# Gated delta attention in a decoder layer: the group's beta in two buffers, the blocks' signs later, squares summed together, w_out scaled on ScalarE, and half of the first inverse on VectorE

## The chip, the core and the metric

The kernel runs on one core of a Trainium2 chip. A core has five engines with instruction lines of their own: TensorE (PE; its weight loads are shown as PEld), VectorE (DVE), ScalarE (ACT), GpSimd (POOL) and SyncE (SP, which issues DMAs here; ACT can issue some too). Each runs its line in order and waits on semaphores for the others. The metric is the device time of one execution in microseconds (us), lower is better. "Span" is the time from the first to the last instruction of the one execution that was profiled.

## What is computed

A decoder layer over 16 sequences (B) of 128 tokens (S) with 256 features: a gated delta attention, a cross attention and a mixture of experts, each followed by a layer norm. All that changes lies in the attention:

```python
mixed = silu(causal_conv4(hidden_states @ w_qkv))      # q, k: 16 heads of 128; v: 32 heads of 128
z     = hidden_states @ w_z
beta  = sigmoid(hidden_states @ w_b)
g     = -exp(A_log) * softplus(hidden_states @ w_a + dt_bias)
q = l2norm(repeat(q, 2)) * 128 ** -0.5                 # 16 heads -> 32
k = l2norm(repeat(k, 2))

def step(Sm, inp):                                     # for each token in turn
    q_, k_, v_, g_, b_ = inp
    Sm = Sm * exp(g_)
    delta = (v_ - einsum('bhk,bhkv->bhv', k_, Sm)) * b_
    Sm = Sm + einsum('bhk,bhv->bhkv', k_, delta)
    return Sm, einsum('bhk,bhkv->bhv', q_, Sm)

og  = o * silu(z)
on  = og * rsqrt(mean(og * og) + 1e-6) * norm_w
x   = layernorm(x + on @ w_out)
```

## The kernel before

**Units and slots.** The recurrence over tokens is done as matrix products. A *unit* is one key head (hk, 16 of them) of one group of G = 4 sequences (g, 4 of them), with its two value heads r = 0, 1: 64 units in all (class Unit). For each unit the 128 tokens are cut into four blocks of 32; within a block a triangular 32x32 matrix has to be inverted, and between blocks there are substitutions. A software pipeline runs over slots `for s in range(NU + DELAY + 3)`. In slot s the unit a = s does its keys and queries (projection pjkq, a convolution over time in ykq, SiLU into kq, the decay scan e from dec, the products pk and lp), v = s - 6 its values (pjv, yv, y2v, vT), m = s - 7 and p = s - 8 their block substitutions (pu) and block products with the inverse (pt), p also its gate (pjz, zs), q = s - 9 the attention (po, og), and o = s - 10 the output (pp, acc).

**Groups and inverses.** Four units with consecutive numbers make a Group (U = 4): 4 units x 2 heads x 4 sequences = 32 blocks in each of four rows of blocks, inverted at once, one block on each partition. `Group.begin` (VectorE) copies the group's beta (bg), transposes it (bp, one buffer), transposes the gathered diagonal blocks (ldg into Tp), and makes nbp = -beta / norm; as its last but one step GpSimd multiplies Tp by nbp (L251), the sign and scale of the blocks. `step(j)`, j = 1 to 30, is two GpSimd operations (L267, L269) on 30 to 240 elements for each partition; `end` sets the diagonal and multiplies by bp (L275); `norms` makes nk (L258); `turn` transposes the result on VectorE into Tt (L279), behind the last lp product of the slot. Group k is inverted in the slots with s // 4 - 1 = k, in the first three of four: each slot has five calls `piece(0)` to `piece(4)`, and the 30 steps are spread over 13 of these 15 pieces. The first pt that uses Tt stands in the slot after.

**Who orders what.** GpSimd's line follows the program text (`manual_schedule` for Pool). The lines of the other engines and of the DMA queues are ordered by a scheduler that estimates times and places an instruction as soon as what it needs is there in that estimate. A buffer's next writer waits for its last reader.

**What stands in a slot, in GpSimd's line:** piece(0); the clear of the lower blocks of lp of unit s - 1 (L417); rstd of o (L478, a power); piece(1), piece(2), the sum of the two conv halves of v (L359, which frees y2v and leads to vT), piece(3), the second such sum, piece(4).

**Sums of squares.** `norms` of a unit squares q (sq), sums over features with a ones matrix into PSUM (pss, L377), transposes (sqt, L380) and makes ss (L382). `rms` does the same for og2 (pms L467, mst L471, var L474, a sum with ss). rstd is var to the power of -0.5, and acc takes pp x rstd.

**w_out.** It has to be scaled by norm_w along rows. `scale_wo(i)`, i = 0 to 7, in slots 2 to 9, loads two heads' rows on SP into a buffer shared with og2, scales on GpSimd (L170) and stores to DRAM (wo_d) on SP; load_o fetches from there.

Of the kernel before, what the change touches and what calls it, by code (L numbers as in the profile page):

```python
# [16 lines left out]
P = 128  # L17
# [24 lines left out]
def decoder_kernel(  # L42
# [16 lines left out]
    ones = const.tile([P, BS], F32, name="ones")  # L59
    pool.memset(ones, 1.0)  # L60
# [56 lines left out]
    with ExitStack() as st:  # L117
# [44 lines left out]
        def scale_wo(i):  # L162

            wor = sb.tile([P, 2, G, P], F32, tag="og2", bufs=1, name=f"wor{i}")
# [49 lines left out]


        NU = NG * HK

        class Group:
# [7 lines left out]
            def begin(self):  # L226
# [11 lines left out]
                self.bp = bp = small("bp", bufs=1)  # L238
# [11 lines left out]

                pool.tensor_tensor(self.T, self.T, bc(nbp[:, None, :], [P, BS, BS]), ALU.mult)  # L251
                sst = small("sst", bufs=1)
                vec.transpose(sst, ss)
                self.sst = sst

# [6 lines left out]
            def step(self, j):  # L262
# [14 lines left out]
            def turn(self, after):  # L277
                self.Tt = sb.tile([P, 8 * U, BS], F32, tag="Tt", name=f"Tt{self.k}")
                inst = vec.transpose(self.Tt.rearrange("p q t -> p t q"), self.T)  # L279
                if after is not None:  # L280
                    tc.add_manual_dep(inst.ins, after.ins.name, mybir.DependencyInfo(
                        mybir.DependencyClass.NoSync, mybir.DependencyReason.DATA),
                        reason="behind what VectorE can do before GpSimd is done")

        class Unit:


            def __init__(self, n):
                self.g, self.hk = divmod(n, HK)
                self.n, self.u = n, n % U  # L290
                self.bt = slice(self.g * G, (self.g + 1) * G)
# [46 lines left out]
            def conv(self, name, ws, chunk, out=None):  # L338
# [10 lines left out]
                for k in (2, 1, 0) if out is not None else (1, 0):  # L349
                    d = 3 - k  # L350
                    vec.scalar_tensor_tensor(  # L351
                        out=y[:, :, d:], in0=pj[:, :, : P - d], scalar=c[:, k : k + 1],
                        in1=y[:, :, d:], op0=ALU.mult, op1=ALU.add)
                if out is not None:
                    act.activation(out, y, AF.Silu)
# [14 lines left out]
            def norms(self):  # L370

                sq = self.t([P], "sq", bufs=1)
                act.activation(sq, self.kq[:, :, 1, :], AF.Square)
                pss = sm_pool.tile([P, G, BS], F32, tag="sm", name=f"pss{self.n}")
                for i in range(NB):
                    blk = slice(i * BS, (i + 1) * BS)
                    pe.matmul(pss[blk].rearrange("p b t -> p (b t)"), lhsT=ones, rhs=sq[:, :, blk],  # L377
                              start=True, stop=True)
                sst = self.t([BS], "sqt", bufs=1)
                vec.transpose(sst, pss)  # L380
                self.ss = self.t([], "ss", bufs=DELAY + 5)
                vec.tensor_scalar(self.ss, sst[:, :, 0], 1e-6, 1e-6 * P, ALU.add, ALU.mult)  # L382

            def decay(self):

                self.e = []
                for r in range(2):
                    e = self.t([P], "e", r)
                    vec.tensor_tensor_scan(  # L389
                        out=e.rearrange("p b t -> p (b t)"), data0=self.dec[:, r, :],  # L390
                        data1=ident4.rearrange("p b t -> p (b t)"), initial=0.0,
                        op0=ALU.mult, op1=ALU.add)
                    self.e.append(e)
# [56 lines left out]
            def attend(self, r):  # L450

                if r == 0:
                    self.og = self.t2("og")
                    self.og2 = self.t2("og2", bufs=1)
# [5 lines left out]
                act.activation(self.og2[:, r], self.og[:, r], AF.Square)  # L460

            def rms(self):

                pms = sm_pool.tile([P, 2, G, BS], F32, tag="sm", name=f"pms{self.n}")
                for i in range(NB):
                    blk = slice(i * BS, (i + 1) * BS)
# [813 lines left out]
```

## Time and profile before

| | us |
|---|---|
| median of 3 runs | 2245.6 (2243.43 to 2249.56) |
| the profiled execution: its time | 2240.06 |
| the profiled execution: its span | 2238.0 |
| start of slot 7 / slot 12 / slot 63 (scan at L389) | 136.8 / 256.8 / 1604.2 |
| w_out's scaling on POOL (L170), 8 times | 22.8 (2.85 each) |
| 480 + 480 operations of the steps on POOL (L267, L269) | 245.6 + 265.8 |
| pss on PE / sqt on DVE / pms on PE / mst on DVE, 64 units | 27.9 / 20.0 / 49.4 / 28.8 |
| granted TensorE clock, mean | 0.969 |

The attention fills the span to about 1800 us; the cross attention and the experts, which the change leaves as they are, follow. In the profile's lists a line reads: place in the kernel and engine, operation, the tile written and those read, shape, count, and in square brackets the idle time just before and what ended it. In the list of waits it reads: the waiting group <- what ended the wait, then total us, number of times and the longest.

### The profile page before, as it was taken

The numbers are of one execution on the slowest core, as the hardware profiler recorded it, in microseconds if no ns is written. First come the engines' busy times: TensorE is split into PE (matmuls) and PEld (weight loads), VectorE is DVE, ScalarE is ACT, GpSimd is POOL, SyncE is SP. The second block draws the span as 40 slices with busy tenths as digits, with TensorE's granted clock in tenths as the row PEclk, the third lists the DMA queues.
The fourth block names the chain that finished last, engine by engine and source line by source line (L and its number), as shares of the span: only waits on it lengthen the run. The fifth ranks groups of instructions, "written<-read, shape, count | busy, mean of one in ns | idle before, by whom it ended". The sixth has DMA issues, their size and how long they took to land. (4 is left out here: it accounts for less than half of the span.)

```text
span 2238.0 us, 41392 instructions
## 1 busy us (share of the span) xinstructions
PE 2063.9 (92%) x15128; PEld 1251.2 (56%) x15128; DVE 1745.9 (78%) x3247; ACT 1331.7 (60%) x2692; POOL 1122.4 (50%) x1679
## 2 busy tenths in 40 slices
PE   5669999999999999999999999999998969999997
PEld 2335555556555655555555556555555634448874
DVE  6757888888898888888888888898866667765545
ACT  4546666666666666666666666666655535554431
POOL 1658374646556473829283746556472143252222
PEclk9879999999999999999999999999999979999998
DMA  6332222222222222222222222222111070013321
GB/s 170 107 104 66 61 60 57 58 62 67 58 67 58 62 57 61 64 62 59 65 57 62 57 58 63 65 58 59 39 32 39 20 259 1 1 52 99 107 85 57
DMA packets 140664, 150.78 MB, mean 67 GB/s; under 512 B 14184, under 2 KB 111472, under 8 KB 140464
## 3 DMA queue, kind: packets, MB, share of 16 engines
q1 hardware_dynamic: 135760, 139.56, 21.7%
q0 software_dynamic: 3072, 8.39, 1.2%
q8 instruction: 122, 2.00, 0.4%
q14 instruction: 78, 0.64, 0.1%
q10 hardware_dynamic: 1632, 0.19, 0.1%
HBM read 125.82 MB, written 22.28 MB: 66 GB/s over the span
## 5 line engine op out<-in xcount | busy, mean ns | idle before, releaser
L523 ACT COPY u<-pt 32x512 f32<-32x512 f32 x512 | 294.9, 576 | 62.6 <-PE pt L519 52.6
L359 POOL TENSOR_TENSOR yv<-yv,y2v 128x508 f32<-128x508 f32 x128 | 162.0, 1265 | 275.2 <-DVE yv L351 269.4
L508 DVE TENSOR_TENSOR u<-u,pu 32x512 f32<-32x512 f32 x384 | 263.6, 686 | 31.1 <-PE pu L504 19.3
L490 DVE SCALAR_TENSOR_TENSOR acc<-pp,rstd,acc 128x256 f32<-128x256 f32 x512 | 222.1, 477 | 83.4 <-POOL rstd L478 79.1
L269 POOL TENSOR_TENSOR Tp<-Tp,tmp 128x30 f32<-128x30 f32 (+14 forms) x480 | 265.8, 554 | 37.6
L486 PE MATMUL pp<-wo,og 128*128 128x256 f32 x1024 | 273.8, 394 | 0.0
L334 PE MATMUL pjkq<-xT,wkq 128*128 128x512 f32 x512 | 244.9, 619 | 25.9 <-issue 20.0
L351 DVE SCALAR_TENSOR_TENSOR ykq<-pjkq,cw,ykq 128x500 f32<-128x500 f32 (+2 forms) x384 | 262.6, 725 | 5.5 <-ACT ykq L344 4.1
L334 PE MATMUL pjv<-xT,wv 128*128 128x512 f32 x512 | 253.2, 617 | 11.0 <-DVE ykq L351 6.6
L334 PE MATMUL pjz<-xT,wz 128*128 128x512 f32 x512 | 249.8, 611 | 12.0 <-DVE yv L351 12.0
L267 POOL TENSOR_TENSOR tmp<-Tp 128x30 f32<-128x30 f32 (+14 forms) x480 | 245.6, 512 | 28.2
L351 DVE SCALAR_TENSOR_TENSOR yv<-pjv,cw,yv 128x504 f32<-128x504 f32 (+1 forms) x256 | 187.9, 734 | 70.3 <-ACT y2v L348 66.2
L486 PEld LDWEIGHTS pp<-wo,og 128*128 128x128 f32 x1024 | 182.6, 189 | 84.7 <-issue 62.2
L519 PE MATMUL pt<-u,Tt 32*32 32x128 f32 x4096 | 175.7, 273 | 19.0 <-DVE u L508 18.5
L519 PEld LDWEIGHTS pt<-u,Tt 32*32 32x32 f32 x4096 | 116.6, 105 | 126.0 <-ACT ykq L344 38.7
L360 ACT ACTIVATE vT<-yv 128x512 f32<-128x512 f32 x128 | 80.3, 627 | 165.1 <-POOL yv L359 165.1
L334 PEld LDWEIGHTS pjkq<-xT,wkq 128*128 128x128 f32 x512 | 93.4, 193 | 142.9 <-issue 124.6
L406 DVE TENSOR_TENSOR lp<-pk,e 128x512 f32<-128x512 f32 x256 | 159.3, 681 | 14.7 <-PE pk L403 14.5
L446 ACT ACTIVATE u<-pv,nk 128x128 f32<-128x128 f32 x512 | 149.7, 370 | 33.0 <-PE pv L443 31.0
L478 POOL TENSOR_TENSOR rstd<-var,m_half 128x8 f32<-128x8 f32 x64 | 105.5, 1649 | 123.1 <-DVE var L474 119.8
L389 DVE TENSOR_TENSOR_SCAN e<-dec,ident 128x512 f32<-128x512 f32 x128 | 162.5, 1310 | 2.3 <-DMA dec<-dec_d 0.6
L457 PE MATMUL po<-lp,u 128*128 128x128 f32 x1024 | 147.8, 285 | 17.1 <-DVE acc L490 17.1
(227 smaller groups left out, 3680.2 us busy)
## 6 DMA issues: line engine op xcount, KB each, us to landing
dec<-dec_d SPq DMA_DIRECT2D x64, 512.0 KB, 5.2
wkq<-in_L_attn_w_qkv_dram SPq DMA_DIRECT2D x128, 128.0 KB, 3.6
wv<-in_L_attn_w_qkv_dram SPq DMA_DIRECT2D x64, 256.0 KB, 2.6
wz<-in_L_attn_w_z_dram SPq DMA_DIRECT2D x64, 256.0 KB, 2.7
wo<-wo_d SPq DMA_DIRECT2D x64, 256.0 KB, 2.7
rx<-xg SPq DMA_DIRECT2D x44, 128.0 KB, 2.1
yg<-ry SPq DMA_DIRECT2D x44, 128.0 KB, 1.7
xg<-zero SPq DMA_DIRECT2D x10, 512.0 KB, 8.0
```

The lines of the kernel that those rows point to most:

```text
L267: pool.tensor_tensor(tv, bc(T[:, j + 1 :, j : j + 1], [P, n, j]), bc(T[:, j : j + 1, 0:j], [P, n, j]), ALU.mult)
L269: pool.tensor_tensor(T[:, j + 1 :, 0:j], T[:, j + 1 :, 0:j], tv, ALU.add)
L334: pe.matmul(pj.rearrange("p b t -> p (b t)"), lhsT=ws[kc], rhs=xTs[self.g][:, kc, :], start=(kc == 0), stop=(kc == 1))
L351: vec.scalar_tensor_tensor(out=y[:, :, d:], in0=pj[:, :, : P - d], scalar=c[:, k : k + 1], in1=y[:, :, d:], op0=ALU.mult, op1=ALU.add)
L359: pool.tensor_tensor(y[:, :, 1:], y[:, :, 1:], y2[:, :, 1:], ALU.add)
L389: vec.tensor_tensor_scan(out=e.rearrange("p b t -> p (b t)"), data0=self.dec[:, r, :], data1=ident4.rearrange("p b t -> p (b t)"), initial ...
L406: self.made = vec.tensor_tensor(self.lp[:, r, hf * 2 : hf * 2 + 2], pk, bc(self.e[r][:, hf * 2 : hf * 2 + 2, None, :], [P, 2, 2, P]), ALU. ...
L486: pe.matmul(pp[:, r, :], lhsT=self.og[:, r, b, :], rhs=self.wo[:, r, :], start=True, stop=True)
L490: vec.scalar_tensor_tensor(out=a, in0=pp[:, r, :], scalar=self.rstd[:, r, b : b + 1], in1=a, op0=ALU.mult, op1=ALU.add)
L508: vec.tensor_tensor(u.u_[r][blk], u.u_[r][blk], pu[blk], ALU.subtract)
L519: pe.matmul(pt[blk, b, :], lhsT=groups[u.n // U].Tt[blk, 8 * u.u + G * r + b, :], rhs=u.u_[r][blk, b, :], start=True, stop=True)
L523: act.copy(u.u_[r][blk], pt[blk])
```

## The change

1. `bp` has two buffers (the pool's default) in place of one.
2. The multiplication of Tp by nbp leaves `begin` and becomes `negate`, called at the next piece; the 30 steps are spread over pieces 1 to 12. rstd so stands ahead of it in GpSimd's line. The clear of lp moves from behind piece(0) to behind piece(3).
3. The squares of q (of the unit in its first slot) and of og share one tile sqs of three parts, and one function `sums` makes one product (psq), one transpose and then var and ss; ss comes one slot later than before. `ones` goes; the scale of ss is changed to fit the mean.
4. w_out is scaled by ScalarE, stored from ScalarE's DMA queue, has a buffer of its own, and is called in slots 5 to 12.
5. For the first group alone (k = 0) the signs and steps 1 to 15 are done on VectorE, steps 16 to 30 on GpSimd, all at the head of slot 4 ahead of `gates([1, 2, 3])`; unit 4's convolution and scan are held behind step 15 in VectorE's line (`behind`).
6. The three later loads of x are called in slots 1 to 3, not ahead of the loop.

```diff
-            wor = sb.tile([P, 2, G, P], F32, tag="og2", bufs=1, name=f"wor{i}")
+            wor = sb.tile([P, 2, G, P], F32, tag="wor", bufs=1, name=f"wor{i}")
...
-            pool.tensor_scalar(wor, wor, normw, None, ALU.mult)
+            act.activation(wor, wor, AF.Copy, scale=normw)
             for k in range(2):
-                nc.sync.dma_start(out=wo_d[2 * i + k], in_=wor[:, k])
+                nc.scalar.dma_start(out=wo_d[2 * i + k], in_=wor[:, k])
...
+        def behind(inst, after):
+            if after is not None:
+                tc.add_manual_dep(inst.ins, after.ins.name, mybir.DependencyInfo(
+                    mybir.DependencyClass.NoSync, mybir.DependencyReason.DATA),
+                    reason="what stands behind another in VectorE's line")
...
-                self.bp = bp = small("bp", bufs=1)
+                self.bp = bp = small("bp")
...
-                pool.tensor_tensor(self.T, self.T, bc(nbp[:, None, :], [P, BS, BS]), ALU.mult)
+                self.nbp = nbp
...
+            def negate(self, eng):
+                eng.tensor_tensor(self.T, self.T, bc(self.nbp[:, None, :], [P, BS, BS]), ALU.mult)
...
-            def step(self, j):
+            def step(self, j, eng):
...
-                pool.tensor_tensor(tv, bc(T[:, j + 1 :, j : j + 1], [P, n, j]),
+                eng.tensor_tensor(tv, bc(T[:, j + 1 :, j : j + 1], [P, n, j]),
                                    bc(T[:, j : j + 1, 0:j], [P, n, j]), ALU.mult)
-                pool.tensor_tensor(T[:, j + 1 :, 0:j], T[:, j + 1 :, 0:j], tv, ALU.add)
+                return eng.tensor_tensor(T[:, j + 1 :, 0:j], T[:, j + 1 :, 0:j], tv, ALU.add)
...
+            def square(self, sqs):
+                act.activation(sqs, self.kq[:, :, 1, :], AF.Square)
...
+        def sums(name, sqs, o, a):
+            lo, hi = (0 if o is not None else 2), (3 if a is not None else 2)
+            psq = sm_pool.tile([P, 3, G, BS], F32, tag="sm", name=f"psq{name}")
+            for i in range(NB):
+                blk = slice(i * BS, (i + 1) * BS)
+                pe.matmul(psq[blk, lo:hi].rearrange("p r b t -> p (r b t)"), lhsT=inv_dv,
+                          rhs=sqs[:, lo:hi, :, blk].rearrange("p r b t -> p (r b) t"),
+                          start=True, stop=True)
+            mst = sb.tile([P, 3, G, BS], F32, tag="mst", bufs=1, name=f"mst{name}")
+            vec.transpose(mst[:, lo:hi].rearrange("p r b t -> p (r b t)"),
+                          psq[:, lo:hi].rearrange("p r b t -> p (r b t)"))
+            if o is not None:
+                o.var = sb.tile([P, 2, G], F32, tag="var", name=f"var{name}")
+                vec.tensor_tensor(o.var, mst[:, 0:2, :, 0], bc(o.ss[:, None, :], [P, 2, G]), ALU.add)
+            if a is not None:
+                a.ss = sb.tile([P, G], F32, tag="ss", bufs=DELAY + 5, name=f"ss{name}")
+                vec.tensor_scalar(a.ss, mst[:, 2, :, 0], 1e-6 / P, 1e-6 * P * P, ALU.add, ALU.mult)
...
-        for g in range(1, NG):
-            load_x(g)
-
...
                     at_ = ph * PIECES + i
-                    total = 3 * PIECES - 2
                     if at_ == 0:
                         inv.begin()
-                    for j in range(1 + 30 * at_ // total, 1 + min(30, 30 * (at_ + 1) // total)):
-                        inv.step(j)
+                    if k == 0:
+                        if at_ == 0:
+                            inv.negate(vec)
+                            for j in range(1, 31):
+                                last = inv.step(j, vec if j <= 15 else pool)
+                                if j == 15:
+                                    a.after = last
+                            inv.norms()
+                            inv.end()
+                        return
+                    if at_ == 1:
+                        inv.negate(pool)
+                    n = 3 * PIECES - 3
+                    if 1 <= at_ <= n:
+                        for j in range(1 + 30 * (at_ - 1) // n, 1 + 30 * at_ // n):
+                            inv.step(j, pool)
                     if at_ == 2 * PIECES - 1:
                         inv.norms()
-                    if at_ == total - 1:
+                    if at_ == n:
                         inv.end()
...
+                if 0 < s < NG:
+                    load_x(s)
                 if s == U:
+                    piece(0)
                     gates([1, 2, 3])
                 if a is not None:
-                    if 2 <= s < 2 + HK // 2:
-                        scale_wo(s - 2)
+                    if U < s <= U + HK // 2:
+                        scale_wo(s - U - 1)
...
-                if o is not None:
-                    o.rms()
+                if o is not None or at(s - 1) is not None:
+                    sums(s, sqs, o, at(s - 1))
+                if a is not None or q is not None:
+                    sqs = sb.tile([P, 3, G, P], F32, tag="og2", bufs=1, name=f"sqs{s}")
                 if a is not None:
                     a.key_query(0)
-                piece(0)
-                if s > 0 and at(s - 1) is not None:
-                    at(s - 1).clear()
+                if s != U:
+                    piece(0)
                 if o is not None:
                     o.rms_end()
...
                 piece(3)
+                if at(s - 1) is not None:
+                    at(s - 1).clear()
```

More of the change, by code (lines that the diff above doesn't have):

```diff
@@ L58, in decoder_kernel @@
     make_identity(nc, ident)
-    ones = const.tile([P, BS], F32, name="ones")
-    pool.memset(ones, 1.0)
     inv_dv = const.tile([P, BS], F32, name="inv_dv")
@@ L278, in turn @@
                 self.Tt = sb.tile([P, 8 * U, BS], F32, tag="Tt", name=f"Tt{self.k}")
[L279 to L283, printed above, removed]
+                behind(vec.transpose(self.Tt.rearrange("p q t -> p t q"), self.T), after)
         class Unit:
@@ L290, in __init__ @@
                 self.n, self.u = n, n % U
+                self.after = None
                 self.bt = slice(self.g * G, (self.g + 1) * G)
@@ L350, in conv @@
                     d = 3 - k
-                    vec.scalar_tensor_tensor(
+                    inst = vec.scalar_tensor_tensor(
                         out=y[:, :, d:], in0=pj[:, :, : P - d], scalar=c[:, k : k + 1],
                         in1=y[:, :, d:], op0=ALU.mult, op1=ALU.add)
+                    behind(inst, self.after)
                 if out is not None:
@@ L368, in key_query @@
                 self.conv(f"kq{i}", ws, chunk, out)
[L370 to L382, printed above, removed]
+            def square(self, sqs):
+                act.activation(sqs, self.kq[:, :, 1, :], AF.Square)
             def decay(self):
@@ L388, in decay @@
                     e = self.t([P], "e", r)
-                    vec.tensor_tensor_scan(
+                    inst = vec.tensor_tensor_scan(
                         out=e.rearrange("p b t -> p (b t)"), data0=self.dec[:, r, :],
@@ L392, in decay @@
                         op0=ALU.mult, op1=ALU.add)
+                    behind(inst, self.after)
                     self.e.append(e)
@@ L447, in values, with attend @@
                 self.u_[r] = v
-            def attend(self, r):
+            def attend(self, r, sqs):
                 if r == 0:
                     self.og = self.t2("og")
-                    self.og2 = self.t2("og2", bufs=1)
                 po = self.bank(f"po{r}")
@@ L459, in attend @@
                 vec.tensor_tensor(self.og[:, r], po, self.zs[r], ALU.mult)
[L460 to L466, printed above, removed]
-                    pe.matmul(pms[blk].rearrange("p r b t -> p (r b t)"), lhsT=inv_dv,
-                              rhs=self.og2[:, :, :, blk].rearrange("p r b t -> p (r b) t"),
-                              start=True, stop=True)
-                mst = sb.tile([P, 2, G, BS], F32, tag="mst", bufs=1, name=f"mst{self.n}")
-                vec.transpose(mst.rearrange("p r b t -> p (r b t)"),
-                              pms.rearrange("p r b t -> p (r b t)"))
-                self.var = var = sb.tile([P, 2, G], F32, tag="var", name=f"var{self.n}")
-                vec.tensor_tensor(var, mst[:, :, :, 0], bc(self.ss[:, None, :], [P, 2, G]), ALU.add)
+                act.activation(sqs, self.og[:, r], AF.Square)
             def rms_end(self):
@@ L540, in decoder_kernel @@
         units[0].load_dec()
-        for g in range(1, NG):
-            load_x(g)
         PIECES = 5
+        sqs = None
         done = None
@@ L610, in decoder_kernel @@
                 if q is not None:
-                    q.attend(0)
+                    q.attend(0, sqs[:, 0])
                 if v is not None:
@@ L625, in decoder_kernel @@
                 piece(3)
+                if at(s - 1) is not None:
+                    at(s - 1).clear()
                 if q is not None:
-                    q.attend(1)
+                    q.attend(1, sqs[:, 1])
                 if p is not None:
@@ L630, in decoder_kernel @@
                 if a is not None:
-                    a.norms()
+                    a.square(sqs[:, 2])
                     a.products(ga)
```

## Prediction

> **What bounds the kernel now.** I read the page's busy times first, then the same by stages (boundaries that I chose at the starts of passes of the loop over s), then the list of waits, then the timeline where the waits point. The page's chain of waits is of no use here: it is followed back only to 1796 us, and all that the change touches lies before that.
>
> ```profile
> PE 2063.9 (92%) x15128; PEld 1251.2 (56%) x15128; DVE 1745.9 (78%) x3247; ACT 1331.7 (60%) x2692; POOL 1122.4 (50%) x1679
> ...
> 60.00:137.00 77.00, 45.16 (x185) 25.70 (x183) 44.37 (x72) 36.02 (x60) 54.62 (x79) 0.81 0.34 97
> 137.00:257.00 120.00, 111.62 (x820) 64.24 (x821) 95.78 (x153) 79.96 (x166) 65.44 (x94) 0.94 0.27 80
> 257.00:1575.00 1318.00, 1259.50 (x10024) 765.52 (x10023) 1141.72 (x1956) 872.13 (x1752) 757.64 (x1119) 0.99 0.22 61
> ```
>
> The columns after the stretch and its length are busy PE, PEld, DVE, ACT, POOL, the granted clock, DMA share and GB/s. From 257 to 1575 us TensorE is busy 1259.5 of 1318.0 us, so a change gains there only what it takes off PE, or the 58.5 us in which PE stands. Before 137 us nothing is full: chains of waits set the pace. So: who makes PE stand?
>
> ```profile
> POOL Tp L251 <- DVE nbp L249: 218.1, 16, 15.8
> DVE acc L490 <- POOL rstd L478: 79.1, 25, 6.1
> DVE bp L239 <- POOL Tp L275: 54.8, 11, 18.1
> ...
> PE pv L443 <- ACT vT L360: 31.2, 14, 14.6
> PE pt L519 <- DVE u L508: 18.5, 32, 1.1
> PE po L457 <- DVE acc L490: 17.1, 13, 1.4
> PE pjz L334 <- DVE yv L351: 12.0, 13, 0.9
> ```
>
> (Total us, times, longest.) Three of PE's waits come 13 or 14 times: once for each group of four slots. A slot is one pass of s; its first DVE work is a scan at L389. Slot 24, a group's first:
>
> ```profile
> 574.92 2.34 DVE L389 TENSOR_TENSOR_SCAN e<-dec,ident 128x512 f32<-128x512 f32 x2
> 578.29 0.15 DVE L474 TENSOR_TENSOR var<-mst,ss 128x8 f32<-128x8 f32 x1
> ...
> 584.16 2.36 POOL L251 TENSOR_TENSOR Tp<-Tp,nbp 128x1024 f32<-128x1024 f32 x1 [14.99 <-DVE nbp L249]
> ...
> 589.11 1.65 POOL L478 TENSOR_TENSOR rstd<-var,m_half 128x8 f32<-128x8 f32 x1
> ...
> 590.79 1.66 DVE L490 SCALAR_TENSOR_TENSOR acc<-pp,rstd,acc 128x256 f32<-128x256 f32 x4 [3.91 <-POOL rstd L478]
> ...
> 592.11 1.16 PE L457 MATMUL po<-lp,u 128*128 128x128 f32 x8 [1.38 <-DVE acc L490]
> ...
> 594.19 1.98 PE L334 MATMUL pjz<-xT,wz 128*128 128x512 f32 x4 [0.92 <-DVE yv L351]
> ...
> 601.38 0.66 PE L443 MATMUL pv<-ident,vT 128*128 128x128 f32 x4 [1.46 <-ACT vT L360]
> ```
>
> The signs of the blocks stand first in POOL's line and wait 15 us for nbp. rstd stands behind them, though its var was there at 578.44: it starts at 589.11, 10.7 us late. VectorE's acc is late with it, then PE's po, pjz and pv, 3.76 us in all. Start-up has another such chain:
>
> ```profile
> 126.93 1.91 POOL L275 TENSOR_TENSOR Tp<-Tp,bp 128x1024 f32<-128x1024 f32 x1
> ...
> 128.88 0.21 DVE L239 STREAM_TRANSPOSE bp<-bg 128x32 f32<-128x32 f32 x1 [18.13 <-POOL Tp L275]
> ...
> 135.00 1.97 DVE L279 STREAM_TRANSPOSE Tt<-Tp 128x1024 f32<-128x1024 f32 x1
> 136.84 2.27 DVE L389 TENSOR_TENSOR_SCAN e<-dec,ident 128x512 f32<-128x512 f32 x2
> ```
>
> VectorE stands 18.1 us, until GpSimd has ended the first inverse; slot 7 begins at 136.8.
>
> **The change, part by part.**
>
> *Signs later: -47 us.* In POOL's line rstd now stands ahead of the signs. It can run from about 578.5 to 580.2, before VectorE comes to acc. The waits removed are po 17.1, pjz 12.0 and pv 31.2 less its one of 14.6 in start-up: 45.7 us; 13 groups x 3.76 is 48.9. I take 47; bounds 0 (if what follows is just as late) and 49. What is late next? GpSimd's inverse starts no later than before, since it waits for the same nbp: its sign takes 2.36, steps 1 to 5 some 4.2, and the first yv is wanted about 16 us into the slot, when it is through. The clear of lp (3 x 0.30) moves behind piece 3, where nobody waits for it within that slot. In slots two and three of a group I get rstd done 5.9 and 6.4 us into the slot, against acc's turn on VectorE at about 6.8 (scans 2.3, mst 0.6, five convs of 0.70, 0.4 small): a margin of under 1 us.
>
> *Beta in two buffers: -12 us.* In the changed program's order of instructions the copy of beta is simply made one group earlier: the bp of group k+2 waits for the end of inverse k (L283), as that of k+1 did. The wait is not gone by the buffer. But bp now stands behind three subtractions (0.69), two convs (0.73) and one acc (0.47) more, 4.0 us, and the ten later waits are (54.8 - 18.1) / 10 = 3.7 us each; the clear no longer stands ahead of L283 either. So they should close, and with them PE's pt waits: 18.5 less some 5.2 in the drain after 1575 us, say 12. Bounds 0 and 13.
>
> *Squares together: -6 us.* Per unit PE loses pss and pms, 27.9 / 64 = 0.436 us and 49.4 / 64 = 0.772 us, and gets one sum over 384 columns: by the same slope 0.772 + 0.336 = 1.11. That is 0.10 x 64 = 6.4 us. Bounds 0 and 11 (0.17 a unit, if the switch between tile shapes costs more than the rows show). VectorE loses a transpose (0.313) and its mst grows from 0.450 to some 0.587: 11 us less, off PE's path.
>
> *w_out on ScalarE: no term of its own.* POOL loses 8 x 2.85 us; ACT gets 8 copies of 128x1024, not in the trace, between 0.6 (the 128x512 copy) and 2.85 (POOL's); I take 1.2, twice the copy, since form and engine are the same. SP loses 16 issues of 0.35 to 0.45 us, ACT gets them at 0.46 to 0.59: 8 us. ACT's cover is its 60% load; without it all 18 us would be added. The order shows the catch: the first scaling stands ahead of the first beta and waits for its load (landed 15.7 us here), so beta, at 13.4 now, comes about 4 us late; and the eight loads stand in SP's line ahead of wkq and dec, each waiting for the store before it. The three later loads of x now stand behind unit 1's wkq, and are wanted only at slot 4.
>
> *First inverse half on VectorE, start-up: +3 us (bounds -13 and +15).* Here I followed the new order by hand. Tp is transposed at about 73 (70.3 now: 4 us late by the above, but unit 4's scan and convs no longer stand ahead). To nbp 4 us, signs 1.3 (2 x the 0.68 of lp's 512 columns), then 30 short operations. 128x32 takes 0.17, 128x128 0.29; the mean of 165 columns gives 0.33, and I allow 0.05 for each waiting on the last: 11.4. The gates' pieces between them are 3.8: the half ends at 93. GpSimd's half is half of (265.8 + 245.6 + 37.6 + 28.2) / 16 = 36 us, then nk 3.0 and the end 2.1: 93 + 18 + 5 = 116, against 128.8 now. But bp of the third group stands in VectorE's line **ahead of unit 4's lp**, and waits for that end. Unit 4's scans and convs are done at 100, so VectorE stands 16 us, with lp of unit 4 and all of units 5 and 6 behind it; now only unit 6's lp is behind the wait. That is 29.6 us of work (lp 3 x 2.5, scans 2 x 2.3, convs 12 x 0.70, yv 4 x 0.73, Tt 1.95, waits for pk 2.6, small ones 1.6): slot 7 at 146, 9 late. Back come some 6 us in slots 7 to 9, where VectorE waits 7.0 and 4.85 us for y2v behind POOL's backlog, of which w_out's 2.85 and the clear go.
>
> PE stands during that wait, which the clock answers. After the 14.6 us wait the next 8 pjkq took 4.81 us, not 3.70, and 8 pjv 6.31, not 3.76: 3.7 us lost. The Trainium skill (TensorE: Matmul & The Clock Gate, What's actually happening) says that an idle window of some 3.4 us halves the clock and a busy one restores it, an estimated loss of 1.7 us for each cold start. By that rule one cold start more would make start-up +4.7; by the rows both kernels have one such stretch, and I add nothing.
>
> The sum: -47 - 12 - 6 + 3 = **-62 us** on the span of 2238.0 (profiled run 2240.06). The median of the runs shown is 2245.6, 5.5 above that run; I apply the sum to the median: **2183 us**.
>
> **Rivals.**
> - *VectorE becomes the bound.* It is busy about 91 us in a group whose PE work is some 98; in its first and third slot 23 to 24. If half of the 47 and half of the 12 go into VectorE's own line: -23 - 6 - 0 + 3 = -26, 2219. For it: its pt waits, which remain in slots with Tt; against: 7 us of slack in a group.
> - *Start-up as meant.* If bp's new place does not hurt, slot 7 moves with the inverse's end, 13 us sooner: -78, 2167. Against it is the order itself.
> - *The second buffer does nothing:* all ten waits stay, -50, 2195.
> - *Slower: GpSimd's line runs late.* Place: rstd in the second and third slot of each group. The steps that stood in slot one behind nbp still fill it, and an instruction of POOL under VectorE's scan took 1.44 us, not 0.65. If rstd is 10 us late there, each costs what the first slot's does now: 2 x 3.76 x 13 = 98 us. Then -47 - 12 - 6 + 3 + 98 = +36, 2281. It decides from about 6 us late in both; against it, my margin has the right sign.
>
> **How the numbers follow.** Forecast 0.60, VectorE bound 0.13, start-up as meant 0.11, no use of the buffer 0.06, slower 0.10. The range runs from 2156 (-49 - 13 - 11 - 13 and a little) to 2222, which takes in the VectorE rival; outside are the slower one and some 0.08 of tails. 0.3% is 6.7 us, what a measurement here can tell from no change: faster 0.86, within 0.04 (tails of the VectorE and the slower rival), slower 0.10.
>
> **What would show it.** Right: in a group's first slot rstd starts within 2 us of var, PE's waits po from acc, pjz from yv and pv from vT fall under 10 us together, POOL's signs still wait some 9 us or more. The long bp wait stands near 100 us, about 16 us long, the others under 1 us. psq costs PE about 71 us. Slot 7's scan near 146. Wrong: rstd late in slots two and three, a new DVE or PE wait that comes 13 times, or ACT standing for w_out's loads with wkq late.

## The result, and the profile after

The changed kernel takes 2189.3 us (median of 4 runs, 2188.7 to 2192.3), the kernel before 2247.1 (4 runs, 2243.4 to 2249.6): a ratio of 0.9747, interval 0.973 to 0.9764. The forecast was 2183, range 2156 to 2222. Two of the seven runs of one experiment below, line_before (2962 and 4833 us), lie far above its other five and are left out. The span went from 2238.0 to 2186.8 us. I cut both spans at the scans of slots 7, 12 and 63, to see which stage the 51.2 us come from:

| stage | before, us | after, us | change | forecast |
|---|---|---|---|---|
| start to slot 7 | 136.8 | 157.5 | +20.7 | +9 |
| slot 7 to 12 | 120.0 | 117.6 | -2.4 | -6 |
| slot 12 to 63 | 1347.4 | 1275.9 | -71.5 | -65 |
| slot 63 to the end | 633.8 | 635.8 | +2.0 | 0 |

So the sum came out 11 us less than forecast on the spans, from two misses of opposite sign: the groups gave more, start-up cost much more. That the total came this near is partly luck. (The forecast's -65 were meant from the first groups on; most of them lie in this stretch.)

The busy times of the changed kernel by stages (columns as in the prediction: busy PE, PEld, DVE, ACT, POOL, granted clock, DMA share, GB/s):

```profile
62.00:157.50 95.50, 51.43 (x195) 28.73 (x192) 59.06 (x111) 39.87 (x66) 27.52 (x47) 0.73 0.31 87
...
275.00:1551.00 1276.00, 1264.20 (x9822) 772.49 (x9821) 1153.42 (x1942) 874.19 (x1793) 765.18 (x1141) 1.00 0.23 64
```

In the stretch from slot 12 to 63 TensorE stands 11.8 us; before it stood 1347.4 - 1287.6 = 59.8. That stretch is now full. The stretch before slot 7 got emptier: 51 of 95 us, at a granted clock of 0.73 where 60 to 137 us of the kernel before had 0.81.

Who makes the engines stand from slot 12 to 63, from the lists of waits of the changed kernel for PE, DVE and POOL (total us, times, longest):

```profile
PE pjv L339 <- issue: 7.0, 13, 0.6
PE pjz L339 <- issue: 3.9, 13, 0.5
...
DVE acc L471 <- POOL rstd L459: 8.4, 13, 0.6
...
POOL Tp L262 <- DVE nbp L254: 50.2, 13, 3.9
```

PE's waits for acc, yv, vT and u are gone; 10.9 us of small ones have come in their place. VectorE's waits for bp are gone too; in the kernel before its list for the same stretch had this line:

```profile
DVE bp L239 <- POOL Tp L275: 36.6, 10, 3.9
```

The reason for the first stands in a group's first slot, again slot 24 (scan at 574.16), on the timeline of the changed kernel:

```profile
577.67 0.15 DVE L490 TENSOR_TENSOR var<-mst,ss 128x8 f32<-128x8 f32 x1
...
577.90 1.65 POOL L459 TENSOR_TENSOR rstd<-var,m_half 128x8 f32<-128x8 f32 x1 [8.60 <-DVE ss L493]
...
582.75 0.49 DVE L471 SCALAR_TENSOR_TENSOR acc<-pp,rstd,acc 128x256 f32<-128x256 f32 x1
...
583.41 2.38 POOL L262 TENSOR_TENSOR Tp<-Tp,nbp 128x1024 f32<-128x1024 f32 x1 [3.87 <-DVE nbp L254]
```

rstd starts 0.1 us after var (10.7 us before the change), is done at 579.55, and acc at 582.75 finds it ready. The signs wait behind it, and nobody waits for them.

Start-up, on VectorE's timeline of the changed kernel:

```profile
80.23 1.98 DVE L246 STREAM_TRANSPOSE Tp<-ldg 128x1024 f32<-128x1024 f32 x1 [1.22 <-ACT ldg L408]
...
99.31 2.70 DVE L384 TENSOR_TENSOR_SCAN e<-dec,ident 128x512 f32<-128x512 f32 x2
...
123.27 0.21 DVE L244 STREAM_TRANSPOSE bp<-bg 128x32 f32<-128x32 f32 x1 [17.37 <-POOL Tp L283]
...
157.53 2.26 DVE L384 TENSOR_TENSOR_SCAN e<-dec,ident 128x512 f32<-128x512 f32 x2
```

The transpose of Tp comes at 80.2, where I had 73; then the half of the inverse until 99.3; then bp of the third group holds VectorE for 17.4 us with unit 4's lp and all of units 5 and 6 behind it, and slot 7 comes 34.3 us after that.

### The profile page after: what moved, and what is told of

Same layout as the page of the kernel before. It is cut to its first block, busy times and chain, and to the rows that moved or that the text cites. A ratio compares the mean times of both kernels' runs of the same rounds, so it can differ in the third digit from the quotient of the medians.

```text
span 2186.8 us, 40366 instructions
## 1 busy us (share of the span) xinstructions
PE 2040.9 (93%) x14688; PEld 1242.5 (57%) x14688; DVE 1740.3 (80%) x3223; ACT 1316.1 (60%) x2696; POOL 1077.0 (49%) x1639
## 4 chain that ended last, share of the span: by engine, by line
PE 72%; POOL 10%; DVE 8%; ACT 4%; issue 3%; DMA 3%; SPq 0%; ACTq 0%; POOLq 0%; DVEq 0%
PE pp L467 9%; PE pjv L339 8%; PE pjz L339 8%; PE pjkq L339 8%; PE pt L520 6%; PE po L452 5%; PE pu L505 5%; PE pk L399 4%; PE psc L787 3%; POOL Tp L277 2%; POOL tmp L275 2%; PE pv L439 2%; PE psq L482 2%; PE prg L1123 2%; PE pru L1123 2%
## 5 line engine op out<-in xcount | busy, mean ns | idle before, releaser
L467 PE MATMUL pp<-wo,og 128*128 128x256 f32 x1024 | 272.1, 395 | 0.0
L277 POOL TENSOR_TENSOR Tp<-Tp,tmp 128x240 f32<-128x240 f32 (+14 forms) x465 | 253.6, 545 | 36.4
L275 POOL TENSOR_TENSOR tmp<-Tp 128x240 f32<-128x240 f32 (+14 forms) x465 | 239.6, 515 | 62.0 <-DVE Tp L277 33.8
L356 DVE SCALAR_TENSOR_TENSOR ykq<-pjkq,cw,ykq 128x504 f32<-128x504 f32 (+2 forms) x384 | 266.2, 725 | 2.8 <-ACT ykq L349 2.3
L471 DVE SCALAR_TENSOR_TENSOR acc<-pp,rstd,acc 128x256 f32<-128x256 f32 x512 | 231.5, 477 | 42.9 <-POOL rstd L459 37.1
L339 PE MATMUL pjz<-xT,wz 128*128 128x512 f32 x512 | 243.7, 598 | 5.9 <-issue 5.9
L452 PE MATMUL po<-lp,u 128*128 128x128 f32 x1024 | 152.2, 285 | 0.0
```

The costliest lines, as they stand in the source:

```text
L275: eng.tensor_tensor(tv, bc(T[:, j + 1 :, j : j + 1], [P, n, j]), bc(T[:, j : j + 1, 0:j], [P, n, j]), ALU.mult)
L277: return eng.tensor_tensor(T[:, j + 1 :, 0:j], T[:, j + 1 :, 0:j], tv, ALU.add)
L339: pe.matmul(pj.rearrange("p b t -> p (b t)"), lhsT=ws[kc], rhs=xTs[self.g][:, kc, :], start=(kc == 0), stop=(kc == 1))
L356: inst = vec.scalar_tensor_tensor(out=y[:, :, d:], in0=pj[:, :, : P - d], scalar=c[:, k : k + 1], in1=y[:, :, d:], op0=ALU.mult, op1=ALU.add)
L452: pe.matmul(po[:, b, :], lhsT=self.u_[r][:, b, :], rhs=self.lp[:, r, b, 1, :], start=True, stop=True)
L467: pe.matmul(pp[:, r, :], lhsT=self.og[:, r, b, :], rhs=self.wo[:, r, :], start=True, stop=True)
```

## The experiments

Twelve kernels, in three sets of four; each set ran on one chip beside runs of the kernel before. All but the last column are from the profiled execution, in us:

| kernel | slot 7 | slot 12 | slots 12 to 63 | rest | time, median |
|---|---|---|---|---|---|
| before | 136.8 | 256.8 | 1347.4 | 633.8 | 2247.1 |
| after | 157.5 | 275.1 | 1275.9 | 635.8 | 2189.3 |
| signs_early | 156.3 | 274.1 | 1299.9 | 638.8 | 2214.5 |
| beta_one | 156.8 | 277.3 | 1275.9 | 635.5 | 2190.0 |
| sums_apart | 158.0 | 276.6 | 1293.1 | 640.2 | 2210.3 |
| wo_pool | 148.7 | 272.1 | 1276.0 | 635.1 | 2185.0 |
| inv_pool | 154.8 | 272.4 | 1276.2 | 657.6 | 2208.3 |
| bp_behind | 146.0 | 263.8 | 1283.4 | 659.1 | 2207.2 |
| wo_late | 148.9 | 270.3 | 1276.7 | 655.8 | 2205.7 |
| both_late | 137.4 | 258.0 | 1282.5 | 661.2 | 2202.3 |
| line_before | 158.5 | 277.2 | 1334.9 | 638.2 | 2255.1 |
| third_wl_inv | 126.8 | 249.4 | 1276.0 | 635.4 | 2163.2 |
| third_wq_inv | 164.4 | 284.7 | 1276.7 | 635.5 | 2198.8 |
| third_wq | 141.3 | 259.3 | 1276.1 | 636.9 | 2178.0 |

The kernel before took 2243.8 in the first set, 2265.0 in the second and 2243.5 in the third. On the chip of the second set the work behind slot 63, which no edit touches, took 656 to 661 us instead of 634 to 640. So I read edits from the first three columns, and times only within a set. The changed kernel itself was not run in these sets; in the first one beta_one, which differs by nothing that shows, stands in for it.

Each place is from one execution. The changed kernel and beta_one, alike in start-up, have slot 7 at 157.5 and 156.8 us and slot 12 at 275.1 and 277.3: there, differences of 1 and 2 us say nothing.

The mean length of a slot in the stretch from slot 12 to 63, in us, by its place in its group of four (13, 13, 13 and 12 slots):

| slot of a group | before | after | signs_early | line_before | sums_apart |
|---|---|---|---|---|---|
| first | 28.31 | 26.15 | 27.86 | 30.42 | 25.91 |
| second | 25.20 | 24.27 | 24.30 | 24.31 | 24.86 |
| third | 28.72 | 26.50 | 26.47 | 26.59 | 26.80 |
| fourth | 23.20 | 23.00 | 23.15 | 23.15 | 23.71 |

The change took as much from the third slots, where bp waited, as from the first, where the signs stand.

**signs_early: the signs alone back ahead of rstd.**

```diff
                     if at_ == 0:
                         inv.begin()
+                        if k > 0:
+                            inv.negate(pool)
...
-                    if at_ == 1:
-                        inv.negate(pool)
```

> The changed kernel, with the signs of groups 1 to 15 again ahead of rstd in GpSimd's line; all else stays. Theory (step A of the prediction): rstd waits again behind the signs, about 9 us into the first slot of a group, and TensorE stands again for acc, yv and vT, some 3.76 us in each of 13 groups: +47 us, near 2236; the trace shows PE waits po from acc, pjz from yv and pv from vT 13 times each. Rival: other parts (squares together, one transpose fewer on VectorE) closed these waits and the signs' place matters little: under +15, below 2204.

The stretch from slot 12 grew by 24.0 us, between the two cases. rstd starts 11.8 us into a group's first slot, not 14.2 as in the kernel before: the change had moved more than the signs past it.

**line_before: signs, first two steps and the clear back ahead of rstd.**

```diff
-                    if at_ == 1:
+                    if at_ == 0:
                         inv.negate(pool)
-                    n = 3 * PIECES - 3
-                    if 1 <= at_ <= n:
-                        for j in range(1 + 30 * (at_ - 1) // n, 1 + 30 * at_ // n):
-                            inv.step(j, pool)
+                    n = 3 * PIECES - 2
+                    for j in range(1 + 30 * at_ // n, 1 + min(30, 30 * (at_ + 1) // n)):
+                        inv.step(j, pool)
...
                 if s != U:
                     piece(0)
+                if at(s - 1) is not None:
+                    at(s - 1).clear()
                 if o is not None:
                     o.rms_end()
...
                 piece(3)
-                if at(s - 1) is not None:
-                    at(s - 1).clear()
```

> The changed kernel with GpSimd's line of groups 1 to 15 as before in full: not only the signs, but steps 1 and 2 and the clear of lp stand again ahead of rstd. (With the signs alone the stretch from slot 12 to slot 63 grew from 1275.9 to 1299.9 us, half of the 47 that step A names.) Theory: the other half lies with the steps and the clear, which moved behind rstd in the same edit: the stretch grows to about 1323 us, and the time is 8 us under the kernel before. Rival: the rest of the 47 came from elsewhere (the sums, the place of bp): the stretch stays near 1300 us, the time about 30 under the kernel before.

The stretch grew by 59.0 us, more than the 47, and the whole kernel is slower than before (ratio 1.0052, interval 1.003 to 1.0074). GpSimd's timeline of line_before in slot 24 (scan at 588.7) shows what stands ahead of rstd:

```profile
598.17 2.37 POOL L262 TENSOR_TENSOR Tp<-Tp,nbp 128x1024 f32<-128x1024 f32 x1 [14.33 <-DVE nbp L254]
600.62 0.25 POOL L275 TENSOR_TENSOR tmp<-Tp 128x30 f32<-128x30 f32 x1
...
602.02 1.02 POOL L413 MEMSET lp<- 32x256 f32 x3
603.13 1.65 POOL L459 TENSOR_TENSOR rstd<-var,m_half 128x8 f32<-128x8 f32 x1
```

var was there 3.7 us into the slot, rstd starts after 14.4. And the waits it makes, from line_before's lists for PE and DVE (from 270 to 1640 us):

```profile
PE pt L520 <- DVE acc L471: 25.8, 13, 2.1
...
DVE acc L471 <- POOL rstd L459: 57.2, 26, 3.9
```

TensorE stands in another place than before (pt for acc, not po), since its order changed too. The mean first slot takes 30.42 us, 26.15 in the changed kernel; the other three differ by under 0.2. Of the 4.27 us TensorE stands 2.76 (3.23 against 0.47), and 1.50 are busy time (27.18 against 25.68). Part of that is matmuls recorded longer in these slots (pjz 666 ns on average against 605, po 305 against 288); TensorE's order differs as well, and how the 1.50 divide is not shown. So the list of waits need not hold all that a late result costs.

The kernel before had the same line of GpSimd, and its first slots took 28.31 us, 2.1 less than here. So the 59.0 us are what the old line costs under the new order of the other engines, not what the change earned by leaving it.

**beta_one: one buffer for bp.**

```diff
-                self.bp = bp = small("bp")
+                self.bp = bp = small("bp", bufs=1)
```

> The changed kernel with one buffer for bp. Only the group index of the copies shifts by one; each stands at the same place in VectorE's line and waits for the same end of an inverse. Theory (step B: it is the place, not the buffer): no change, 2185 to 2193, and the wait of 17 us near 106 us of the span stays. Rival (the buffer itself earned the 12 us): +12, near 2201, with ten bp waits of about 3.7 us each.

No change: 1275.9 us in the stretch, 2190.0 in all. The buffer by itself does nothing. In the changed kernel and in this one bp stands 14.7 us into the third slot, when the inverse has ended at 13.3. Before, it stood in line from 9.4 us on and waited until 13.0. Three subtractions, two convs and one acc that followed it now stand ahead of it, as the prediction had read. The place is what closed the wait.

What the wait cost is seen in the kernel before: it comes in ten of the thirteen third slots, and in three (26, 42 and 58) bp stands in the slot after and does not wait. From first slot to first slot, the nine whole groups with the wait took 105.9 us on average and the three without it 104.2; after the change the same groups take 99.7 and 100.7. Those with it gained 6.2 us each and those without 3.5, so the wait was worth 2.7 us a group, some 27 in all. The two kinds are not quite alike otherwise, as the second pair of numbers shows; this is an estimate.

**sums_apart: the sums of the squares in two sets again.**

```diff
-                    sums(s, sqs, o, at(s - 1))
+                    sums(s, sqs, o, None) if o is not None else None
+                    sums(f"k{s}", sqs, None, at(s - 1)) if at(s - 1) is not None else None
```

> The changed kernel with the sums of the squares in two sets of matmuls and two transposes again (keys 128 columns, outputs 256). The prediction priced this at 0.10 us of TensorE a unit: +6, near 2195. From the changed kernel's trace the price is 0.32 us a unit (0.424 + 0.794 before, 0.902 now): +20, near 2209. Rival: VectorE's extra transpose (0.31 us a unit) lands on its line where it has no slack, and costs as much again: +40, near 2229.

20.3 us above beta_one, and 17.2 in the stretch. Its matmul groups there (busy us, mean ns, then idle before them and who ended it):

```profile
L482 PE MATMUL psq<-sqs,inv_dv 128*32 128x256 f32 x408 | 34.4, 391 | 0.0
L482 PE MATMUL psqk<-sqs,inv_dv 128*32 128x128 f32 x408 | 21.7, 285 | 10.0 <-DVE mst L486 9.0
```

and the one group of the changed kernel:

```profile
L482 PE MATMUL psq<-sqs,inv_dv 128*32 128x384 f32 x408 | 46.0, 498 | 0.0
```

34.4 + 21.7 against 46.0 is 10.1 us, 0.20 for each of the 51 units; 10.0 more are a wait of the second set, nearly all of it for VectorE's transpose of the first, because both use the one bank of that tag. The total I expected was right; half of it is the wait, not the matmuls. That wait belongs to this kernel, where the two sets stand one behind the other. The kernel before had none there (the 0.0 at the end of the lines):

```profile
L467 PE MATMUL pms<-og,inv_dv 128*32 128x256 f32 x408 | 40.5, 391 | 0.0
L377 PE MATMUL pss<-sq,ones 128*32 128x128 f32 x408 | 21.7, 285 | 0.0
```

Against it the change saves 62.2 - 46.0 = 16.2 us of matmuls, 0.32 for each unit.

**wo_pool: w_out on GpSimd in slots 2 to 9 again.**

```diff
-            act.activation(wor, wor, AF.Copy, scale=normw)
+            pool.tensor_scalar(wor, wor, normw, None, ALU.mult)
...
-                nc.scalar.dma_start(out=wo_d[2 * i + k], in_=wor[:, k])
+                nc.sync.dma_start(out=wo_d[2 * i + k], in_=wor[:, k])
...
-                    if U < s <= U + HK // 2:
-                        scale_wo(s - U - 1)
+                    if 2 <= s < 2 + HK // 2:
+                        scale_wo(s - 2)
```

> The changed kernel with w_out scaled on GpSimd in slots 2 to 9 again, its stores in SyncE's queue. Theory: in the changed kernel the eight loads of w_out stand in SyncE's queue ahead of wkq and dec of the first units, each behind the store before it, and the scalings ahead of the first beta on ScalarE; without them Tp of the first group is transposed near 71 us (now 80.2), slot 7's scan comes near 148 (now 157.5), and the time is near 2180. Rival (prediction: no term of its own; start-up is late only for the wait of bp): slot 7 within 3 us of 157.5 and the time 2187 to 2194.

Slot 7 comes 8.8 us sooner and Tp of the first group at 68.9, but slots 7 to 12 give 5.8 back (123.4 us instead of 117.6): two of the eight scalings stand there on GpSimd, at 167.5 and 195.1, which may be the reason. The time is 5.0 us under beta_one's. What the change does to SyncE's queue is seen on the timeline of the changed kernel:

```profile
42.15 0.89 SPq L166 DMA_DIRECT2D wor<-in_L_attn_w_out_dram  x2
43.15 0.40 SPq L316 DMA_DIRECT2D dec<-dec_d  x1
43.65 0.93 SPq L311 DMA_DIRECT2D wkq<-in_L_attn_w_qkv_dram  x2
```

and on TensorE's:

```profile
56.21 2.04 PE L339 MATMUL pjkq<-xT,wkq 128*128 128x512 f32 x2 [17.22 <-issue]
```

From 32 to 42 us the queue issued nothing: the third load of w_out waited for the second store, which was issued at 32.0 and 32.3 and landed at 41.5 and 42.1, and dec and wkq stood behind it; this wkq had landed by 53.0. TensorE stood 17.2 us, until 56.2. What released it the profile does not name.

**inv_pool: the first inverse wholly on GpSimd.**

```diff
-                            inv.negate(vec)
+                            inv.negate(pool)
                             for j in range(1, 31):
-                                last = inv.step(j, vec if j <= 15 else pool)
-                                if j == 15:
-                                    a.after = last
+                                inv.step(j, pool)
```

> The changed kernel with the first inverse wholly on GpSimd (signs and steps 1 to 30); the place of beta's copies stays. GpSimd needs about 36 us for the 30 steps and 2.4 for the signs, so from nbp at 83.7 the inverse ends near 128 instead of 123.3; unit 4's scans and convs need not wait for VectorE's half any more. Theory (step E: what stands behind bp in VectorE's line sets slot 7): slot 7 some 5 us later, near 162, time near 2194. Rival (the half on VectorE is what made start-up late): slot 7 back near 140, time near 2172.

Neither: slot 7 2.7 us sooner. VectorE had nothing of the inverse to do, took unit 4's scan at 77.3, and then stood at bp for 26.4 us until 126.6, where the inverse had ended. What the half saves on GpSimd it takes from VectorE.

**bp_behind: each group's bp behind the scans of its own first slot.**

```diff
-                vec.transpose(bp, bg)
+                behind(vec.transpose(bp, bg), after)
...
                     behind(inst, self.after)
+                    self.scan = inst
...
-                        inv.begin()
+                        inv.begin(a.scan if k > 0 and a is not None else None)
```

> The changed kernel with each group's bp transposed behind the scans of its own group's first slot, so that no bp stands ahead of unit 4's lp. Theory (step E): the 17 us wait near 106 us goes, lp of unit 4 and the work of units 5 and 6 run while GpSimd works; slot 7's scan comes near 140 (now 157.5) and the time near 2172; nothing changes in the steady groups. Rival (GpSimd's end or the loads set slot 7 anyway): slot 7 within 5 us of 157.5, time 2184 to 2190.

Slot 7 comes 11.5 us sooner, so bp's place is a cause; I had hoped for 17, but one of unit 4's convs now waits 4 us for ScalarE, which the wait of bp had covered. The stretch from slot 12 to 63 loses 7.5 us, which I had put at nothing: bp now stands in a group's first slot, right ahead of Tp's transpose. That this is what costs it is an argument, not shown.

**wo_late: the loads of w_out held behind dec of the next unit.**

```diff
-                nc.sync.dma_start(out=wor[:, k], in_=w_out[hk * 256 : (hk + 1) * 256, :]
-                                  .rearrange("(r p) n -> p r n", p=P))
+                behind(nc.sync.dma_start(out=wor[:, k], in_=w_out[hk * 256 : (hk + 1) * 256, :]
+                                         .rearrange("(r p) n -> p r n", p=P)), after)
...
-                nc.sync.dma_start(
+                self.dec_load = nc.sync.dma_start(
                     out=self.dec,
...
-                        scale_wo(s - U - 1)
+                        scale_wo(s - U - 1, at(s + 1).dec_load)
```

> The changed kernel with the loads of w_out held in SyncE's queue behind dec of the next unit, so that they really stand in slots 5 to 12. Theory: they leave the queue of the first units, beta and the first wkq and dec come as before; Tp of the first group near 71 us (now 80.2), slot 7's scan near 148, time near 2180. Rival: within 3 us of 2189, since the wait of bp stays and sets slot 7; or w_out's later stores make the first load of wo late and the gain goes in slots 9 to 13.

Slot 7 8.6 us sooner, as with wo_pool; slot 12 4.8 sooner. This and wo_pool agree on what the early loads cost.

**both_late: the edits of bp_behind and wo_late together.**

> Both edits: w_out's loads held behind dec, and bp behind the scans of its own slot. Theory: the two delays of start-up add, slot 7's scan near 130 and the time near 2161, below both kernels. Rival: they hide one another and only the larger counts, near 2172.

They add: 8.6 and 11.5 make 20.1, and slot 7 comes 20.1 us sooner, at 137.4. It is still 7 us later than I expected; the half of the inverse stands on VectorE ahead of units 4 to 6.

**third_wl_inv: three edits to start-up.** Those of wo_late and inv_pool, and bp held behind the scans for the third group alone:

```diff
-                        inv.begin()
+                        inv.begin(a.scan if k == 2 else None)
```

> The changed kernel with three edits to start-up: bp of the third group alone behind the scans of its own slot, w_out's loads held behind dec, and the first inverse wholly on GpSimd. Theory: VectorE is free of 15 us of signs and steps, units 4 to 6 are done near 108, and the inverse, from Tp near 71, ends near 118: slot 7's scan near 122 (137.4 with the half on VectorE, 157.5 in the changed kernel), the time some 80 us under the kernel before on the same chip (the changed kernel: 54 to 58 under). Rival: GpSimd's backlog (clears, yv of slots 7 to 9) eats it: slot 7 early, but slot 12 no earlier than 258, some 68 under.

80.3 us under the kernel before: 2163.2 us, ratio 0.9643, interval 0.9623 to 0.9664, the fastest kernel here. From VectorE's timeline of third_wl_inv:

```profile
104.45 2.73 DVE L384 TENSOR_TENSOR_SCAN e<-dec,ident 128x512 f32<-128x512 f32 x2
```

This is unit 6's scan, and its convs are done before the inverse ends at 118.3. Slot 7 comes 10.6 us sooner than in both_late, and the steady groups are as short as in the changed kernel. Slots 7 to 12 take 122.6 us, 5 more than in the changed kernel; part of the rival came true.

**third_wq_inv: w_out on GpSimd and its own queue in slots 0 to 3.** third_wl_inv's other two edits stay; w_out's becomes:

```diff
-                nc.sync.dma_start(out=wor[:, k], in_=w_out[hk * 256 : (hk + 1) * 256, :]
+                nc.gpsimd.dma_start(out=wor[:, k], in_=w_out[hk * 256 : (hk + 1) * 256, :]
...
-            act.activation(wor, wor, AF.Copy, scale=normw)
+            pool.tensor_scalar(wor, wor, normw, None, ALU.mult)
...
-                nc.scalar.dma_start(out=wo_d[2 * i + k], in_=wor[:, k])
+                nc.gpsimd.dma_start(out=wo_d[2 * i + k], in_=wor[:, k])
...
-                    if U < s <= U + HK // 2:
-                        scale_wo(s - U - 1)
+                    if s < U:
+                        scale_wo(2 * s)
+                        scale_wo(2 * s + 1)
```

> As the run before, but w_out is loaded, scaled and stored by GpSimd and its own queue in slots 0 to 3, where GpSimd has little to do, instead of ScalarE from slot 5. Theory: slots 7 to 12, which took 120 to 123 us with w_out's work in them, take 117 again: some 84 us under the kernel before. Rival: the loads crowd those of x, wkq and dec in the first 40 us, or GpSimd's own issues make the identity late: slot 0's scan 3 us or more after 33, no better than the run before.

A miss, and for a reason neither case named: 35.6 us slower than third_wl_inv. Slot 0's scan is at 33.4, so nothing is crowded. GpSimd's timeline of third_wq_inv:

```profile
89.02 1.45 POOL L166 DMA_DIRECT2D wor<-in_L_attn_w_out_dram  x2 [2.44 <-DMA wo_d<-wor]
...
113.81 2.35 POOL L262 TENSOR_TENSOR Tp<-Tp,nbp 128x1024 f32<-128x1024 f32 x1
```

Eight rounds of load, scale and store, each waiting for the store before it, take 10 to 18 us each and last until 112.7. The first inverse stands behind them in GpSimd's line and starts 41 us later than in third_wl_inv (72.7).

**third_wq: the same with the half on VectorE** (inv_pool's edit left out).

> As the run before, but with the change's half of the first inverse on VectorE. Theory: slot 7 near 137 again, since 15 us of VectorE's line stand ahead of units 4 to 6: 15 us slower than the run before, some 69 us under the kernel before. Rival: the half on VectorE brings the inverse's end forward, and that is what slot 7 waits for: within 3 us of the run before, or faster.

20.8 us faster than third_wq_inv, the opposite of the theory, as the rival had it: with GpSimd blocked until 112.7, signs and 15 steps on VectorE shorten what is late. Whether the half pays depends on which engine is behind.

## Why the prediction held, step by step

The three terms of the groups came to -65, and the stretch gave -71.5. That is partly luck: one term was too large and two were too small.

*Signs later, -47: mechanism right, term too large.* The waits named are gone, and the rival that needed a late rstd in slots two and three did not happen. But the first slots gained 2.16 us each, 28 in all (2.85 and 37 if they are cut where TensorE begins pjkq), and not 13 x 3.76. Once the squares and beta's wait are taken from the 71.5, some 28 us are left for the signs with the steps and the clear (71.5 - 16.2 - 27, an estimate). Undone within the changed kernel they cost 59.0, of which the signs alone 24.0 and steps 1 and 2 with the clear the rest; that is dearer than the same line was in the kernel before. The step that failed is taking TensorE's listed waits as gained in full: TensorE does stand 2.91 us less in a first slot (3.38 before, 0.47 now), but its busy time there rose from 24.93 to 25.68, since 8.2 of the pjkq products now fall into it on average, 6.8 before. The narrow margin was real: rstd is done 6.0 and 7.1 us into slots two and three (I had 5.9 and 6.4), acc comes at 6.8 and 7.2, and in slot three VectorE waits 0.64 us.

*Two buffers for beta, -12 (bounds 0 and 13): the reading of the order was right, the term too small.* The buffer earns 0.0. The ten waits closed because bp stands later, as the step said, and that was worth some 27 us by the groups with and without the wait. The step priced TensorE's listed pt waits only; the waits themselves, 36.6 us of VectorE, were the nearer guide. No kernel I ran has the old place (bp_behind has a third one, 7.5 us dearer), so this rests on the comparison within the kernel before. Which edit made the scheduler move bp is open: in beta_one, signs_early, line_before and sums_apart it stands 14.7 to 15.2 us into these slots, so no edit undone there brings it back by itself.

*Squares together, -6: too small.* It is 16.2 us by the matmuls against the kernel before, and 17.2 in the stretch of sums_apart. The sum over 384 columns costs 0.90 us a unit, not the 1.11 drawn from the slope of narrower ones.

*w_out on ScalarE, no term of its own: wrong.* The prediction saw the loads "in SP's line ahead of wkq and dec, each waiting for the store before it" and priced only beta, 4 us (beta came at 18.8 us, 5.4 late). It cost 8.6 to 8.8 us at slot 7; the 3.0 to 4.8 at slot 12 stand little above the 2.2 by which kernels that are alike differ there.

*First inverse half on VectorE, start-up, +3 (bounds -13 and +15): the step that failed.* It was +18.3 at slot 12, outside its bounds. The long bp wait stands as foretold (17.4 us, I had 16) but at 106, not 100, since w_out's loads made Tp late; and the work behind it took 34.3 us, not 29.6. The -6 in slots 7 to 9 were -2.4 up to slot 12. Of the 15 us by which the step was wrong, some 7 are Tp's transpose, for which it had counted no more of w_out's loads than beta's delay, 5 the work behind bp, and the rest the smaller gain behind slot 7. At slot 7 the parts are 8.6 for w_out's loads, 11.5 for bp's place (these add), and some 10.6 for the half itself once the other two are mended, against 2.7 while bp still waits.

On the clock: TensorE's long stands in start-up were 10.9 and 14.6 us before, and are 17.2 and 17.6 now. Behind the last of these two pjkq took 2.05 us (four took 1.99 at 151.9) and eight pk 3.78 (1.89 at 149.7), at a granted clock of 0.50: 2.9 us lost. The 3.7 us that the prediction read behind the 14.6 us stand of the kernel before were two slow stretches, not one: right behind the stand pv took 1.11 us instead of some 0.60 and pjkq 4.81 instead of 3.70, 1.6 lost; then the granted clock was 1.00 from 137 to 140 us, and the slow pjv at 142.5 came when it had fallen to 0.50 once more. So this stand lost 1.6 us before and 2.9 now. What all slow stretches of start-up cost together was not measured. The Trainium skill (TensorE: Matmul & The Clock Gate, What's actually happening) has the clock halved after an idle window and restored by a busy one; the doubled times agree with a halved clock. The 1.7 us that I estimated from that page fit the stand of the kernel before and are too few for the changed kernel's, and the measurement decides.

The rivals: VectorE did not become the bound (its waits remain, TensorE is 99% busy in the stretch); start-up as meant did not happen in the change, and bp's place is part of why, as foretold (with three edits more it did, in third_wl_inv); the second buffer does nothing as a buffer, but the waits closed nevertheless. Of what was named beforehand as showing the forecast right, three things missed: GpSimd's signs wait 3.9 us, not 9 or more, because rstd now runs in the time in which they would have waited; psq costs 61.0 us, not 71; and slot 7's scan is at 157.5, not 146. Of what was to show it wrong, ScalarE did stand for w_out's loads, 24.3 us in all, with wkq late.

## What to carry to other kernels

In an engine's line that runs in order, ask of every instruction that waits what stands behind it: moving the few things that wait (signs, first steps, a clear) behind a tiny result that was ready earned some 28 us, moving one 0.2 us transpose behind work that was ready some 27, and the same transpose hoisted ahead of its need in start-up cost 11.5. Undoing an edit prices it in the new order, which can be dearer than what it earned: 59.0 us against some 28 here. A kernel in which a wait comes in some groups and not in others prices that wait by itself. The scheduler here put a load where its buffer, not its slot number, allowed it, so a late place in the program must be held by an order of its own. Splitting work onto a second engine pays only while the first one is what is late: at slot 7 the same half cost 10.6 us, cost 2.7 and saved 23 in three surroundings.

## What was not expected of the hardware

In line_before a first slot shows 27.18 us of busy TensorE, in the changed kernel 25.68, with the pjz matmuls recorded at 666 and 605 ns: time that TensorE loses there seems to be recorded in part as busy, though its order differs too. And the part behind the attention took 634 to 640 us on the chip of the first and third set and 656 to 661 on that of the second, where the kernel before was slower by as much (2265.0 us against 2243.8): times of different sets can't be set side by side without the kernel before.
